# A causal penalty that waits in PSUM: ScalarE presets the diagonal blocks, and the scores come in three pieces

## The chip, the core and the metric

The kernel runs on one core of a Trainium2 chip. Its time is the device time of one execution in microseconds (us). The engines are named as in the profile: PE is TensorE (PEld its weight loads), DVE is VectorE, ACT is ScalarE, POOL is GpSimd, and SP issues most of the DMAs. A weight load and its product are two records each for a 32-bit product, because such a product runs in two passes; a 16-bit product and a transpose run in one.

## What is computed

The input x is 4 sequences of 512 tokens with 128 features. A first block adds ordinary causal attention to it, and six layers of local attention with feed-forward parts follow. The change touches only the first block:

```python
x = x + attn(layernorm(x), Wq, Wk, Wv, Wr)
# inside attn: 16 heads of 64
scores = SCALE * einsum('bqhd,bkhd->bhqk', q, k)
causal = triu(ones((s, s)), k=1)
scores = scores + MASK_PENALTY * causal        # -50 where key > query
attn = softmax(scores, axis=-1)
out = einsum('bhqk,bkhd->bqhd', attn, v)       # then @ Wr
```

The penalty is finite, so keys ahead of the query keep a small weight and all 512 keys are scored for each query.

## The kernel before

**Tiles and slots.** The first stage works on row blocks. A block (class `Rows`) is one sequence `b`, one pair of heads `c` (8 pairs) and one quarter `t` of the queries (4 quarters of 128): 128 blocks in all, each a PSUM tile `ps_sc` of 128 x 2 heads x 512 keys in 32 bit, which fills two banks. There are two such tiles (`bufs=2`), so block n writes the tile that block n-2 had. A loop over `m` handles two blocks in each of 64 slots: even slots have the quarters 0 and 1, odd slots the quarters 2 and 3. The order on every engine is the order of the calls in this loop (lines 422 to 493), written out by hand.

**A slot on PE.** (1) `times_v1` (L393): attention times v, half of it for an older pair of heads, from m = 4 on. (2) `scores` for both blocks (L308): for each block two halves of 256 keys by two heads, each head on its own 64 rows of the array; the two heads' products run beside each other. (3) `penalty` (L323): for each block and head one 16-bit product of an identity (`ident16`) with the mask `pen` adds the penalty to the block's own 128 x 128 square, the only one that the diagonal crosses. (4) In odd slots `make_v` (L287). (5) `transposes` (L373) of the first block of the slot before, 4 for each head. (6) `make_q` (L271, even) or `make_k` (L277, odd). (7) The transposes of the second block of the slot before. The q, k and v products and the layer norm share the one bank `ps_pj`.

**The other engines in a slot.** DVE takes the row maximum of a block over all 512 keys (L335, 128x1024), and a second bias for the squares behind the diagonal, whose penalty is constant (`bias`, L339; not for quarter 3). ACT takes the exponents (L348): for each head the keys up to the diagonal square, and the rest with the other bias; each is followed by a read of the accumulated sum. POOL normalises (L362). ACT copies the first head's transposes to SBUF and DVE the second's (L377, L381). ACT also copies v (L294) and q (L273), DVE copies k (L279) and, in odd slots, the finished head pair `aT` (L403).

ACT's order in a slot is: v (odd slots), first block's transposes of the slot before, exponents of the first block, exponents of the second, q (even slots), the second block's transposes of the slot before. DVE's is: `aT` (odd slots), first maximum, its bias, transposes, second maximum, its bias, k (odd slots), sums and reciprocals.

**Even slots with more work.** For the layer norm of the next sequence and of the residual, even slots hold a mean (L109, L111, L113), a variance (L118, L120) or a scaling (L126, L130): six slots of each kind. Thirteen even slots from m = 8 on hold none of these and are called plain here. Three odd slots also hold a projection of 16 products (L407).

**The start.** SP issues the loads of x's first half, `ident16`, `pen`, then x of the second sequence (L200), and further loads; wq, wk and wv are issued by ACT. PE transposes the second sequence (`load_x(1)`, L224) before 16 warming products (L239) and the first q.

Only these calls of the loop matter for what follows, in this order:

```python
times_v1(g // NC, g % NC, odd)           # m >= 4
for r in now: r.scores()
for r in now: r.penalty()
now[0].maximum()                         # then v, norm steps, bias
old[0].transposes()
now[0].exponents()                       # then now[1].maximum(), bias
now[1].exponents()                       # then the copies of q and of the transposes
```

Of the kernel before, what the change touches and what calls it, by code (L numbers as in the profile page):

```python
# [8 lines left out]
F32 = mybir.dt.float32  # L9
# [6 lines left out]
P = 128  # L16
# [4 lines left out]
NC = INNER // P  # L21
# [11 lines left out]
def body(ctx: ExitStack, tc: tile.TileContext, a, out: bass.AP):  # L33
# [5 lines left out]
    nc = tc.nc  # L39
    x = a["x"]  # L40
    B, S, _ = x.shape
# [18 lines left out]
    tabs = const.tile([P, NT, 4, HD], F32, tag="tabs", name="tabs")  # L60
    band = const.tile([P, 2, 2 * W], BF16, tag="band", name="band")
    ident16 = const.tile([P, P], BF16, tag="ident16", name="ident16")
# [99 lines left out]
    s1 = steps[0].enter_context(tc.tile_pool(name="s1", bufs=1))  # L162
    ps1t = steps[0].enter_context(tc.tile_pool(name="ps1t", bufs=1, space=PSUM, side="right"))
    ps1 = step0.enter_context(tc.tile_pool(name="ps1", bufs=1, space=PSUM))
# [25 lines left out]
    with tc.manual_schedule():  # L190
# [2 lines left out]
        wv = s1.tile([P, INNER], F32, tag="wv", name="wv")  # L193
        wr = s1c.tile([P, NC, EMB], F32, tag="wr", name="wr")
        pen = s1.tile([P, P], BF16, tag="pen", name="pen")
        xr = [s1.tile([P, NT, EMB], F32, tag="xr", name=f"xr{b}", bufs=2) for b in range(B)]
        for b in range(B):
            src = x[b].rearrange("(t p) e -> p t e", p=P)
            if b:
                nc.sync.dma_start(out=xr[b], in_=src)  # L200
            else:
                nc.sync.dma_start(out=xr[b][:, 0:2], in_=src[:, 0:2])
                nc.scalar.dma_start(out=xr[b][:, 2:NT], in_=src[:, 2:NT])
                nc.sync.dma_start(out=ident16, in_=a["ident16"])
                nc.sync.dma_start(out=pen, in_=a["pen"])
        for t_, n_ in ((wq, "wq"), (wk, "wk"), (wv, "wv")):
            nc.scalar.dma_start(out=t_, in_=a[n_])
        nc.sync.dma_start(out=wr, in_=a["wr"].rearrange("(c p) e -> p c e", p=P))
# [58 lines left out]
        qs, ks, vs, pTs, os_, aTs = {}, {}, {}, {}, {}, {}  # L267
# [28 lines left out]
        class Rows:  # L296


            def __init__(self, b, c, t):
                self.b, self.c, self.t = b, c, t  # L300

            def scores(self):
                b, c, t = self.b, self.c, self.t
                sc = self.sc = ps1.tile([P, 2, S], F32, tag="sc", name="ps_sc", bufs=2)
                for k0 in range(0, S, S // 2):
                    for h in range(2):
                        rows = slice(h * HD, (h + 1) * HD)
                        mm(  # L308
                            sc[:, h, k0 : k0 + S // 2],
                            lhsT=qs[b, c][rows, t * P : (t + 1) * P],  # L310
                            rhs=ks[b, c][rows, k0 : k0 + S // 2],
                            start=(k0 == 0),
                            stop=False,
                            skip_group_check=True,
                        )

# [67 lines left out]
        def times_v1(b, c, half):  # L384

            if half == 0:
                os_[b, c] = ps1b.tile([P, S], F32, tag="o1", name="ps_o1", bufs=1)
            o = os_[b, c]
            for k in (2 * half, 2 * half + 1):
                for h in range(2):  # L390
                    col = (2 * c + h) % HEADS * HD
                    j, col = col // 512, col % 512
                    mm(  # L393
                        o[h * HD : (h + 1) * HD, :],
                        lhsT=vs[b, j][:, k, col : col + HD],
                        rhs=pTs[b, c][:, h, k, :],
                        start=(k == 0),
                        stop=(k == NT - 1),
                        skip_group_check=True,
                    )  # L400
            if half == 1:
                at = aTs[b, c] = s1c.tile([P, S], F32, tag="aT1", name="aT1", bufs=NC + 2)
                nc.vector.tensor_copy(at, o)  # L403

        def project_out1(b, y):
            for c in range(NC):
# [5 lines left out]
        rows = [Rows(b, c, t) for b in range(B) for c in range(NC) for t in range(NT)]  # L412
# [8 lines left out]
        last = len(rows) // 2  # L421
        for m in range(last):
            b, c, odd = m // (2 * NC), m // 2 % NC, m % 2
            now = rows[2 * m : 2 * m + 2]
            old = rows[2 * m - 2 : 2 * m] if m else []
            if m >= 4:
                g = m // 2 - 2
                times_v1(g // NC, g % NC, odd)
            for r in now:
                r.scores()  # L430
            for r in now:
                r.penalty()
            if m in (2, 3):
                load_x(m)

            scale = None
            if not odd and c == 3 and b + 1 < B:
                scale = norms[b + 1][2]
            if b in range(1, B) and not odd and c == 6:
                scale = norms1[b - 1][2]  # L440
            if scale:
                scale()
            if now:
                now[0].maximum()
            if m < 2:
                make_v(0, 0, 2 * m)
                make_v(0, 0, 2 * m + 1)
            if odd and c < NT:
                make_v(b, 1, c)
            elif odd and b + 1 < B:  # L450
                make_v(b + 1, 0, c - NT)
            if not odd and 1 <= c <= 2 and b + 1 < B:
                if c == 1:
                    norms[b + 1] = norm_x(b + 1)
                norms[b + 1][c - 1]()
            if b in range(1, B) and not odd and 4 <= c <= 5:
                norms1[b - 1][c - 4]()
            if now:
                now[0].bias()
            if old:  # L460
                old[0].transposes()
            out_ = b > 0 and c == 1 and odd
            if now:
                now[0].exponents()
                if not out_:
                    now[1].maximum()
                    now[1].bias()

            bn, cn = (b, c + 1) if c + 1 < NC else (b + 1, 0)
            copies = []  # L470
            if bn < B:
                copies.append((make_k if odd else make_q)(bn, cn))
            if out_ and now:
                now[1].maximum()
                now[1].bias()
            if now:
                now[0].inverse()
                now[0].normalise()
            if old:
                copies.append(old[1].transposes(later=True))  # L480
            if now:
                now[1].exponents()
            for f in copies:
                f()
            if now:
                now[1].inverse()
                now[1].normalise()
            if out_:
                y = bank1()
                project_out1(b - 1, y)  # L490
                residual1(b - 1, y)
                norms1[b - 1] = norm_x1(bank1, b - 1)
            if b == B - 1 and c == 2 and not odd:
                start = shifted(0), layer_tables(0)
# [393 lines left out]
    def first_slot():  # L888


        new = units[0]
        part[0] = 2
        times_v1(B - 1, NC - 2, 0)
        do_project(new, 0)
        do_project(new, 1)
        rows[-2].transposes()
        rows[-1].transposes(later=True)()
        first_step()
        square(new, 0)
        times_v1(B - 1, NC - 2, 1)  # L900
        rotate(new, 0)
        sum_squares(new, 0)
        add_rotated(new, 0)
        times_v1(B - 1, NC - 1, 0)
        square(new, 1)
        rotate(new, 1)
        sum_squares(new, 1)
        add_rotated(new, 1)
        guard(new)
        nc.scalar.preload_act_table_set("natural_log_exp_and_others")  # L910
        inverse_norms(new)
        times_v1(B - 1, NC - 1, 1)
        second_step()
        over_norm(new, 0)
        over_norm(new, 1)
        do_project(new, 2)
        keep_v(new)
# [89 lines left out]
    with tc.manual_schedule():  # L1007
# [14 lines left out]
        for n in range(NT, end - NT, NT):  # L1022
            f = Ffn(units[n - 1], eng=nc.gpsimd, later=later)
# [26 lines left out]
        last = Ffn(units[end - 1], NT - 1, 1, big, sixths, nc.gpsimd)  # L1050
# [53 lines left out]
def _constants(n):  # L1104
# [4 lines left out]
    f = np.float32  # L1109
    half = np.arange(0, HD, 2, dtype=f)  # L1110
    inv_freq = (f(1.0) / np.power(f(10000.0), half / f(HD))).astype(f)
    t = np.arange(n, dtype=f)
# [8 lines left out]
    def by_token(lo, hi):  # L1121
# [3 lines left out]
    tabs = np.stack(  # L1125
        [
            by_token(cos * scale, cos * scale) * f(8.0),
            by_token(-sin * scale, sin * scale) * f(8.0),
            by_token(cos * inv, cos * inv),
            by_token(-sin * inv, sin * inv),  # L1130
        ],
        axis=2,
    )

    q = np.arange(W)[:, None]
    k = np.arange(2 * W)[None, :] - W
    seen = (q >= k) & (q <= k + W)
    band = np.zeros((P, 2, 2 * W), f)
# [3 lines left out]
    band = band.astype(ml_dtypes.bfloat16)  # L1142
# [1 line left out]
    pen = np.where(np.arange(P)[None, :] > np.arange(P)[:, None], PEN, 0.0).astype(ml_dtypes.bfloat16)  # L1144
    ident16 = np.eye(P).astype(ml_dtypes.bfloat16)
    zeros = np.zeros((W, 2, NC, HD + 1), f)
    return {"tabs": tabs, "band": band, "pen": pen, "ident16": ident16, "zeros": zeros}


# [49 lines left out]
```

## Time and profile before

| What | Value |
|---|---|
| Median of 3 runs | 2070.51 us (2067.06 to 2072.57) |
| The profiled execution: its own time | 2072.4 us |
| Its span, first to last instruction | 2070.6 us |
| Mean granted TensorE clock | 0.996 |
| PE busy in the span | 2028.4 us (98%) |
| ACT busy | 1368.2 us (66%) |
| DVE busy | 1640.8 us (79%) |
| POOL busy | 1316.5 us (64%) |
| First scores to last scores of the first stage | 23.5 us to 524.8 us |
| L323 (penalty) PE busy | 25.4 us, 256 records |
| L308 (scores) PE busy | 129.1 us, 1024 records |

PE's busy time counts a product's latency too, and products overlap, so a busy PE isn't at its peak. The profiled execution lies 1.8 us above its span and 1.9 us above the median of the runs.

### The profile page before, as it was taken

How to read it: one execution, taken by the hardware profiler on the slowest of the kernel's cores; microseconds unless marked ns; L12 is line 12 of the kernel's file. 1: busy time of each engine (PE TensorE's matmuls, PEld its weight loads, DVE VectorE, ACT ScalarE, POOL GpSimd, SP SyncE). 2: the span in 40 equal slices, each digit the busy share in tenths (PEclk: the TensorE clock that was granted, in tenths of full speed). 3: DMA queues.
4: the chain of work that ended last, by engine and by line, in shares of the span. 5: the costliest groups of instructions: out<-in, count | busy, mean ns of one | idle time of the engine just before them, and what ended most of it. 6: DMA issues, size and time to landing. Idle time of an engine off the chain costs nothing.

```text
span 2070.6 us, 77263 instructions
## 1 busy us (share of the span) xinstructions
PE 2028.4 (98%) x34382; PEld 1329.1 (64%) x34382; DVE 1640.8 (79%) x2240; ACT 1368.2 (66%) x2678; POOL 1316.5 (64%) x1432
## 2 busy tenths in 40 slices
PE   7999999999999999999999999999999999999998
PEld 5665555655466666666666666666666666666665
DVE  3766766767698888888888888888888888888885
ACT  3665665666455766676776676776667776677763
POOL 1554554555677677667767667667677767667762
PEclk8999999999999999999999999999999999999999
DMA  3000000000011121111211112111121111211110
GB/s 127 1 1 1 1 1 1 1 1 1 12 44 36 42 67 44 44 44 33 77 44 34 54 36 64 53 35 44 46 64 44 38 51 46 67 41 44 38 45 27
DMA packets 34968, 77.44 MB, mean 37 GB/s; under 512 B 4686, under 2 KB 18764, under 8 KB 34636
## 3 DMA queue, kind: packets, MB, share of 16 engines
q1 hardware_dynamic: 33932, 70.79, 11.8%
q8 instruction: 272, 4.46, 0.9%
q10 hardware_dynamic: 704, 1.70, 0.2%
q14 instruction: 60, 0.49, 0.1%
HBM read 23.50 MB, written 1.05 MB: 12 GB/s over the span
## 4 chain that ended last, share of the span: by engine, by line
PE 91%; DVE 5%; ACT 2%; POOL 1%; issue 1%; DMA 0%; SPq 0%; POOLq 0%; ACTq 0%
PE ps_proj L548 23%; PE ps_one L661 12%; PE ps_one L762 7%; PE ps_att L737 7%; PE ps_sc L308 6%; PE ps_o L393 6%; PE ps_att L700 5%; PE ps_pt L373 5%; PE ps_proj L812 3%; PE ps_proj L813 3%; PE ps_proj L832 3%; PE ps_pj L287 1%; PE ps_att L690 1%; PE ps_pj L277 1%; PE ps_pj L271 1%; PE ps_pj L407 1%
## 5 line engine op out<-in xcount | busy, mean ns | idle before, releaser
L587 POOL TENSOR_TENSOR rot<-rot,t 128x1024 f32<-128x1024 f32 x192 | 454.2, 2366 | 232.6 <-DVE t L576 220.1
L548 PE MATMUL ps_proj<-wqkv,xs 128*128 128x512 f32 x1152 | 569.0, 602 | 0.5 <-PE ps_one L661 0.2
L362 POOL TENSOR_TENSOR pr<-pr,den 128x1024 f32<-128x1024 f32 x128 | 241.0, 1893 | 248.3 <-DVE den L359 238.5
L606 POOL TENSOR_TENSOR rot<-rot,ss 128x1024 f32<-128x1024 f32 x192 | 361.3, 1903 | 7.4
L560 ACT ACTIVATE sq<-ps_proj 128x1024 f32<-128x1024 f32 x192 | 196.4, 1023 | 93.8 <-PE ps_proj L548 93.6
L548 PEld LDWEIGHTS ps_proj<-wqkv,xs 128*128 128x128 f32 x1152 | 188.2, 190 | 102.0 <-issue 92.1
L570 DVE TENSOR_TENSOR rot<-ps_proj,lt 128x1024 f32<-128x1024 f32 x192 | 233.3, 1215 | 10.2 <-ACT sq L560 10.0
L576 DVE TENSOR_TENSOR t<-ps_proj,lt 128x1024 f32<-128x1024 f32 x192 | 232.9, 1213 | 0.0
L348 ACT ACTIVATE pr<-ps_sc,nm 128x128 f32<-128x128 f32 (+3 forms) x448 | 220.3, 509 | 11.8 <-DVE nm L335 8.6
L565 DVE TENSOR_REDUCE ss<-sq 128x16 f32<-128x1024 f32 x192 | 221.1, 1190 | 0.0
L661 PEld LDWEIGHTS ps_one<-ident,rot 128*128 128x128 f32 x1536 | 172.7, 141 | 61.2 <-issue 51.2
L661 PE MATMUL ps_one<-ident,rot 128*128 128x128 f32 x1536 | 205.1, 276 | 1.1 <-POOL xs L170 0.6
L335 DVE TENSOR_REDUCE nm<-ps_sc 128x2 f32<-128x1024 f32 x128 | 155.9, 1218 | 62.9 <-PE ps_sc L323 62.8
L664 ACT COPY pT<-ps_one 128x512 f32<-128x512 f32 x192 | 110.0, 587 | 136.6 <-PE ps_one L661 136.6
L762 PEld LDWEIGHTS ps_one<-aT,wo 128*128 128x128 f32 x1536 | 182.9, 192 | 23.6 <-issue 17.7
L762 PE MATMUL ps_one<-aT,wo 128*128 128x128 f32 x1536 | 189.1, 276 | 0.3 <-ACT tmp_t L852 0.2
L746 DVE RECIPROCAL rden<-ps_att 128x8 f32<-128x8 f32 x192 | 38.8, 202 | 176.8 <-PE ps_att L737 176.7
L648 ACT COPY vt<-ps_proj 128x512 f32<-128x512 f32 x192 | 103.1, 590 | 96.4 <-PE ps_proj L548 96.4
L373 PEld LDWEIGHTS ps_pt<-ident,pr 128*128 128x128 f32 x1024 | 117.4, 142 | 58.5 <-issue 47.4
L664 ACT COPY qT<-ps_one 128x512 f32<-128x512 f32 x192 | 103.1, 589 | 66.1 <-PE ps_one L661 66.1
L377 ACT COPY pT<-ps_pt 128x512 f32<-128x512 f32 x128 | 75.6, 591 | 98.0 <-PE ps_pt L373 98.0
L373 PE MATMUL ps_pt<-ident,pr 128*128 128x128 f32 x1024 | 135.9, 274 | 3.0 <-DVE pT L381 2.4
(178 smaller groups left out, 3763.2 us busy)
## 6 DMA issues: line engine op xcount, KB each, us to landing
vs<-vt SPq DMA_DIRECT2D x96, 390.0 KB, 3.7
vs<-vt SPq DMA_DIRECT2D x72, 130.0 KB, 3.6
wqkv<-in_wqkv_dram SPq DMA_DIRECT2D x18, 512.0 KB, 4.0
vs<-in_zeros_dram SPq DMA_DIRECT2D x24, 130.0 KB, 3.7
wo<-in_wo_dram SPq DMA_DIRECT2D x6, 512.0 KB, 4.2
w<-in_w_dram SPq DMA_DIRECT2D x6, 341.0 KB, 5.9
xr<-in_x_dram SPq DMA_DIRECT2D x3, 256.0 KB, 7.6
scales<-in_scales_dram SPq DMA_DIRECT2D x6, 128.0 KB, 3.1
```

Source lines behind the costliest of these rows:

```text
L348: nc.scalar.activation(self.pr[:, h, cols], self.sc[:, h, cols], AF.Exp, bias=self.nm[:, part_, h : h + 1], accum_out=self.den[:, part_, h ...
L362: nc.gpsimd.tensor_tensor(self.pr, self.pr, self.den[:, 0].unsqueeze(2).to_broadcast([P, 2, S]), ALU.mult)
L373: nc.tensor.transpose(pt[:, k * P : (k + 1) * P], self.pr[:, h, k * P : (k + 1) * P], ident)
L548: mm(p[:, c, :], lhsT=u.xs[:, u.T * P : (u.T + 1) * P], rhs=wpart[j][:, c * 512 : (c + 1) * 512], start=True, stop=True,)
L565: nc.vector.tensor_reduce(u.ss[:, j * HEADS : (j + 1) * HEADS], heads(u.sq[j]), AX.X, ALU.add)
L570: nc.vector.tensor_tensor(heads(t0), heads(pf), lt[:, u.T, 2 * j].unsqueeze(1).to_broadcast([P, HEADS, HD]), ALU.mult)
L576: nc.vector.tensor_tensor(t1.rearrange("p (h t d) -> p h t d", t=2, d=half), pf.rearrange("p (h t d) -> p h t d", t=2, d=half)[:, :, ::-1, :],
L587: nc.gpsimd.tensor_tensor(u.r[j], u.r[j], u.t1, ALU.add)
L606: nc.gpsimd.tensor_tensor(heads(u.r[j]), heads(u.r[j]), u.ss[:, j * HEADS : (j + 1) * HEADS].unsqueeze(2).to_broadcast([P, HEADS, HD]), AL ...
L661: nc.tensor.transpose(tp[:, c * P : (c + 1) * P], src[:, (4 * g + c) * P : (4 * g + c + 1) * P], ident)
L664: nc.scalar.copy(dst[:, 4 * g : 4 * g + 4, col0 : col0 + P], tp.rearrange("p (c t) -> p c t", c=4))
L762: mm(y[:, 0:P], lhsT=wo_w[0][:, k, :], rhs=u.aT[:, g].rearrange("p (j f) -> p j f", f=P)[:, :, f0 : f0 + W], start=(k == 0), stop=(k == NC ...
```

## The change

A 32-bit copy of the mask, `pen32`, is loaded by SP right after `pen`, ahead of x of the second sequence. From the second slot on, ACT copies it into the own square of both heads of a block's PSUM tile (`preset`, one instruction of 128x256 for each block) one slot ahead: for the first block of the next slot right after the exponents of the first block of this slot, and the same for the second. Both take the tile whose exponents ACT has just read. The scores then start with the own square, adding to what lies there, and go on with the two squares of the other half of the keys and the square beside the own one: pieces of 128, 256 and 128 keys, instead of 256 and 256. The 16-bit products stay in the first slot (m = 0) only, whose scores are also in three pieces. In odd slots the copy of `aT` moves behind the first maximum on DVE. The file's second half is unchanged but for a call of the function that `times_v1` now returns.

```diff
+        pen32 = s1.tile([P, P], F32, tag="pen32", name="pen32")
...
                 nc.sync.dma_start(out=pen, in_=a["pen"])
+                nc.sync.dma_start(out=pen32, in_=a["pen32"])
...
-                self.b, self.c, self.t = b, c, t
+                self.b, self.c, self.t, self.sc = b, c, t, None
+
+            def preset(self):
+                sc = self.sc = ps1.tile([P, 2, S], F32, tag="sc", name="ps_sc", bufs=2)
+                nc.scalar.copy(
+                    sc[:, :, self.t * P : (self.t + 1) * P], pen32.unsqueeze(1).to_broadcast([P, 2, P])
+                )
 
             def scores(self):
                 b, c, t = self.b, self.c, self.t
-                sc = self.sc = ps1.tile([P, 2, S], F32, tag="sc", name="ps_sc", bufs=2)
-                for k0 in range(0, S, S // 2):
+                own = self.sc is not None
+                if not own:
+                    self.sc = ps1.tile([P, 2, S], F32, tag="sc", name="ps_sc", bufs=2)
+                sc, far = self.sc, (1 - t // 2) * 2
+                for k, (k0, n) in enumerate(((t, 1), (far, 2), (t ^ 1, 1))):
+                    cols = slice(k0 * P, (k0 + n) * P)
                     for h in range(2):
                         rows = slice(h * HD, (h + 1) * HD)
                         mm(
-                            sc[:, h, k0 : k0 + S // 2],
+                            sc[:, h, cols],
                             lhsT=qs[b, c][rows, t * P : (t + 1) * P],
-                            rhs=ks[b, c][rows, k0 : k0 + S // 2],
-                            start=(k0 == 0),
-                            stop=False,
+                            rhs=ks[b, c][rows, cols],
+                            start=(k == own),
+                            stop=own or k == 2,
                             skip_group_check=True,
                         )
...
             if half == 1:
                 at = aTs[b, c] = s1c.tile([P, S], F32, tag="aT1", name="aT1", bufs=NC + 2)
-                nc.vector.tensor_copy(at, o)
+                return lambda: nc.vector.tensor_copy(at, o)
+            return lambda: None
...
-                times_v1(g // NC, g % NC, odd)
+                keep = times_v1(g // NC, g % NC, odd)
             for r in now:
                 r.scores()
-            for r in now:
+            for r in now if m == 0 else ():
                 r.penalty()
...
             if now:
                 now[0].maximum()
+            if m >= 4:
+                keep()
...
                 now[0].exponents()
+                if m + 1 < last:
+                    rows[2 * m + 2].preset()
...
                 now[1].exponents()
+                if m + 1 < last:
+                    rows[2 * m + 3].preset()
```

## The prediction

> **What bounds the kernel now.** The page first: one engine is nearly full.
>
> ```profile
> PE 2028.4 (98%) x34382; PEld 1329.1 (64%) x34382; DVE 1640.8 (79%) x2240; ACT 1368.2 (66%) x2678; POOL 1316.5 (64%) x1432
> ```
>
> Busy is not bound, so the second view is the busy time by stretches of 14.50 us, one even and one odd plain slot.
>
> ```profile
> 99.21:113.71 14.50, 14.50 (x96) 8.79 (x95) 10.46 (x21) 10.14 (x34) 7.88 (x5) 1.00 0.01 2
> ```
>
> PE has no gap, at full clock; ACT (fifth figure) has 4.4 us to spare. The timeline of PE shows the steps: scores, penalty and transposes start when the step before lets them.
>
> ```profile
> 104.25 2.00 PE L308 MATMUL ps_sc<-k,q 64*128 64x256 f32 x16
> 106.19 0.40 PE L323 MATMUL ps_sc<-pen,ident 128*128 128x128 bf16 x4
> 106.42 1.04 PE L373 MATMUL ps_pt<-ident,pr 128*128 128x128 f32 x8
> ...
> 111.04 2.00 PE L308 MATMUL ps_sc<-k,q 64*128 64x256 f32 x16
> 112.97 0.40 PE L323 MATMUL ps_sc<-pen,ident 128*128 128x128 bf16 x4
> 113.20 0.65 PE L287 MATMUL ps_pj<-wv,xnT 128*128 128x512 f32 x1
> ```
>
> ACT's timeline of the same even slot runs late: the exponents end at 111.70, after the next scores have begun at 111.04.
>
> ```profile
> 107.06 0.58 ACT L377 COPY pT<-ps_pt 128x512 f32<-128x512 f32 x1 [2.52 <-PE ps_pt L373]
> 107.83 0.37 ACT L348 ACTIVATE pr<-ps_sc,nm 128x128 f32<-128x128 f32 x1 [0.18 <-DVE nm L335]
> ...
> 109.55 0.21 ACT L348 ACTIVATION_READ_ACCUMULATOR pr<-ps_sc,nm 128x1 f32 x1
> 109.77 0.47 ACT L348 ACTIVATE pr<-ps_sc,nm 128x256 f32<-128x256 f32 x1
> ...
> 111.49 0.21 ACT L348 ACTIVATION_READ_ACCUMULATOR pr<-ps_sc,nm 128x1 f32 x1
> ```
>
> Those scores' second block needs the tile that these exponents read. After an even slot with a mean the timeline shows the wait:
>
> ```profile
> 170.18 2.13 PE L308 MATMUL ps_sc<-k,q 64*128 64x256 f32 x16
> 170.87 0.24 ACT L348 ACTIVATION_READ_ACCUMULATOR pr<-ps_sc,nm 128x1 f32 x1
> 171.17 0.73 PEld L308 LDWEIGHTS ps_sc<-k,q 64*128 64x128 f32 x8 [0.26 <-ACT pr L348]
> ```
>
> The load starts 0.05 after the read's end, 0.99 after the first score, and the scores take 2.13, not 2.00. So a load up to 0.86 after the first score costs nothing. The plain slot is ready at 111.70 + 0.05 = 111.75 against 111.04 + 0.86 = 111.90: a slack of 0.15, which is what the change spends.
>
> **PE: the penalty goes.** In even slots the penalty's first load starts at 106.18 and the transposes at 106.42: 0.24. Without it their own load, hidden now behind the penalty, lies open: 0.05, by L393, whose loads are as long (136 ns against 142) and whose first product of a group takes 645 ns, not 592. Saved: 0.19. In odd slots v follows 0.23 after the penalty's load, its second record comes 0.06 later than spacing asks, and an open load of 128 32-bit columns costs 0.11 (first score 481 ns, others 376): 0.18. At 0.19, over 63 slots, **-12.0 us**.
>
> **PE: three pieces.** The columns stay the same, but four record steps of a block are 128 wide. Their price is that of a step whose weights change each time:
>
> ```profile
> 1009.51 1.95 PE L762 MATMUL ps_one<-aT,wo 128*128 128x128 f32 x16
> ```
>
> The steps there are 0.11 apart, the load hidden, against 0.215 for 256 columns: 0 to 0.02 us more for a block; I take 0.01, 128 times: **+1.3**. The Trainium skill, "TensorE: Matmul & The Clock Gate", section "The mechanism", speaks against the pieces: a weight load overlaps running products only in another row group. By it a narrow step would be load plus stream, 0.21, and the sum 55 us worse; the row above shows the overlap within one row group.
>
> **ACT: the preset's price.** No row has ACT writing PSUM. The nearest are copies from SBUF:
>
> ```profile
> L804 ACT COPY rot<-xT x1: 298/298/298, 2048.6 to 2048.6; 64x128 f32<-64x128 f32 x1
> ```
>
> With 107 ns for 128 more columns (L113 takes 310 ns at 128 and 524 at 384) that is 0.40; it holds ACT for 0.31, as instructions overlap by 0.09. The farthest rows are 0.23 (128x32) and 0.68 (512-wide exponents). The Trainium skill, "ScalarE: Activation LUTs", section "Step-by-step: what each stage is for", says that ACT reaches PSUM faster than SBUF, without a figure; every 0.1 us saved would take 6.6 us off the sum below.
>
> The preset also waits for ACT's own last read: in the changed kernel's instruction list it carries a wait on ACT. Such a wait costs 0.03:
>
> ```profile
> 607.63 0.23 ACT L598 ACTIVATE y<-ss 128x32 f32<-128x32 f32 x1 [2.47 <-POOL ss L590]
> 607.89 0.23 ACT L599 ACTIVATE y<-y 128x32 f32<-128x32 f32 x1
> ```
>
> So a preset delays what is queued behind it: after a read's start ACT goes on at 0.21 + 0.03 + 0.31 = 0.55 instead of 0.09: +0.46. And PE is released by the second preset's end, 0.03 + 0.40 = 0.43 later than by the read.
>
> **The plain even slot.** The first maximum no longer waits for both blocks and the penalty: it starts about 1.2 after the first score, not 2.25. The first exponents then wait only for the copy of the transposes (107.06, 0.19 earlier) and its 0.48: 107.35, so 0.48 earlier. The second exponents gain 0.48, lose 0.46, and lose a wait of 0.14 for their bias (109.64 to 109.77), whose maximum comes earlier too: 0.16 earlier. Ready: 111.75 - 0.16 + 0.43 = 112.02. Needed: 111.90 - 0.19 = 111.71. **PE stalls 0.31**, in the odd slot that follows.
>
> The same sum for the others, each from its own slack:
> - Variance (6): slack 0.44, exponents only 0.19 earlier, bias wait 0.09: 0.19 - 0.46 + 0.09 makes them 0.18 later; stall 0.18 + 0.43 + 0.19 - 0.44 = 0.36.
> - Scaling (6): L130 still precedes the maximum, so 0.19 earlier; bias wait 0.14, 0.13 later, slack 0.15: stall 0.60.
> - Mean (5): the exponents come 0.30 earlier, as L111 no longer follows a late maximum; 0.16 later, no slack, 0.13 lost already: 0.78 added.
> - The first three slots wait for ACT already: 0.87 added each.
>
> Sum: 13 x 0.31 + 6 x 0.36 + 6 x 0.60 + 5 x 0.78 + 2.6 = **+16.3**.
>
> Odd slots: their exponents end at 118.57 and the next slot's scores start at 118.76, so the second block's load has a slack of 118.76 + 0.86 - 118.62 = 1.00. The 0.19 and the stall move both sides, since the first exponents there follow v and the transposes; 0.46 + 0.43 leave 0.11, no stall. If that cover is gone, each 0.1 costs 3 us.
>
> **Edits at nothing.** Behind the second preset lie the copies of q and of transposes; q is copied about 0.5 us before v needs its bank. The `aT` copy moves ahead of the first bias in odd slots: 0.67, but that bias is ready 0.8 before ACT asks (ACT waits for v there); its bank is next written after the following slot has begun. POOL starts an even slot's second block at 112.67 for 1.89, 1.4 before its transposes at 115.92, and moves by under 0.5; an odd slot's second waits for its first on POOL anyway (118.05 to 121.79, transposes at 122.7).
>
> **The start.** `pen32` goes ahead of the second sequence on SP. PE waits 3.96 us for that load now, and it stays ahead of warming and q. One issue costs 0.45, its 64 KB 0.2 of the DMA flow: 0.2 to 0.7, I take **+0.5**.
>
> **Sum:** -12.0 + 1.3 + 16.3 + 0.5 = +6.1 on the profiled execution's 2072.4 (span 2070.6): 2078.5. That execution lies 1.9 above the median, so 2076.6.
>
> **Rivals.**
> - *The preset is covered* (faster): ACT has 4.4 us free in 14.5 and four presets ask 1.8; if release came 0.31 earlier, PE would stay the bound: -12.0 + 1.3 + 0.5 = -10.2, 2060.3. Against it: the free time lies after the exponents, the slack was 0.15, and 2.13 at 170.18 shows the wait. It needs a release within 0.1 us of the read.
> - *The preset is dear* (slower): a PSUM write as slow as the 512-wide exponents, 0.68, adds 0.28 twice in 33 slots: +18.5, 2095. It decides from 0.41 on. Against it: copies are cheaper than exponents.
> - *Narrow loads lie open* (slower): 4 x 128 steps at 0.107 are +55, while a slower PE takes 12 to 16 us of stalls away: about 2117. Against it: the 0.11 steps.
> - Whether PE adds to the preset or overwrites it changes no time.
>
> **The numbers.** A measurement of this kernel tells 0.3%, or 6.2 us, from no change. The forecast has 0.74; presets of 0.34 to 0.45, steps and start at their ends put it at 2070 to 2084, half beyond 6.2: slower 0.37, same 0.37. Covered: 0.13, faster. Dear: 0.08; open loads: 0.05, both slower. Faster 0.13, same 0.37, slower 0.50. The range takes in the covered case and ends at 2085.
>
> **What would show it.** Right: 126 presets of 0.40; the penalty left in the first slot alone; score steps of 0.11; the first maximum 1.2 after the first score; odd slots whose second block waits for the preset, 0.3 after plain slots, 0.6 after scalings and 0.9 after means; even slots without a wait. Wrong: two plain slots in 14.12 (covered), scores over 2.3 without a wait (open loads), waits in even slots.

## The result, and the profile after

The changed kernel takes 2080.07 us (median of 8 runs, 2076.15 to 2083.36) against 2070.41 for the kernel before beside it (8 runs, 2067.06 to 2075.39): a ratio of 1.0042, 95% interval 1.0027 to 1.0056. It is slower, by 5.6 to 11.6 us (the interval times 2070.41). The prediction had 2076.6 in a range of 2059 to 2085, with "slower" as the likeliest of the three outcomes. The profiled execution took 2081.23 us, its span is 2079.4, and its mean granted clock 0.993 (before: 0.996).

The page after shows what became of the chain that ended last. Before, PE had 91% of it and ACT 2%:

```profile
PE 2029.2 (98%) x34642; PEld 1343.3 (65%) x34642; DVE 1640.6 (79%) x2240; ACT 1415.8 (68%) x2804; POOL 1316.5 (63%) x1432
...
PE 83%; ACT 8%; DVE 5%; issue 1%; POOL 1%; DMA 0%; SPq 0%; POOLq 0%; ACTq 0%
```

PE's busy time did not fall, although 252 products left it, for rows like the 2.36 and the half clock below count as busy. ACT's share of the chain is the new thing. The windows of the same kind of two plain slots as before (one even, one odd) give 14.47 us, where before had 14.50:

```profile
111.84:126.31 14.47, 14.40 (x104) 9.06 (x102) 10.57 (x20) 11.57 (x39) 7.53 (x5) 1.00 0.01 1
```

The timeline of PE in those slots answers to the rows of L308, L323 and L373 before. The penalty is gone and the transposes start 1.96 behind the first score; the odd slot's scores take 2.36 (second fence), not the 2.02 of the even slot:

```profile
111.84 2.02 PE L322 MATMUL ps_sc<-k,q 64*128 64x128 f32 x24
113.80 1.09 PE L387 MATMUL ps_pt<-ident,pr 128*128 128x128 f32 x8
114.72 1.02 PE L273 MATMUL ps_pj<-xnT,wq 128*128 128x512 f32 x2
115.58 1.04 PE L387 MATMUL ps_pt<-ident,pr 128*128 128x128 f32 x8
```

```profile
118.42 2.36 PE L322 MATMUL ps_sc<-k,q 64*128 64x128 f32 x24
```

ACT's timeline and PE's weight loads there show why. The last read ends at 118.97 + 0.21 = 119.18, the preset starts 0.03 later and ends at 119.21 + 0.38 = 119.59, and the second block's first load follows at 119.63:

```profile
116.69 0.22 ACT L362 ACTIVATION_READ_ACCUMULATOR pr<-ps_sc,nm 128x1 f32 x1
116.94 0.38 ACT L308 COPY ps_sc<-pen 128x256 f32<-128x256 f32 x1
117.25 0.47 ACT L362 ACTIVATE pr<-ps_sc,nm 128x256 f32<-128x256 f32 x1
...
118.97 0.21 ACT L362 ACTIVATION_READ_ACCUMULATOR pr<-ps_sc,nm 128x1 f32 x1
119.21 0.38 ACT L308 COPY ps_sc<-pen 128x256 f32<-128x256 f32 x1
```

```profile
118.42 0.96 PEld L322 LDWEIGHTS ps_sc<-k,q 64*128 64x128 f32 x12 [0.81 <-issue]
119.63 0.96 PEld L322 LDWEIGHTS ps_sc<-k,q 64*128 64x128 f32 x12 [0.26 <-ACT ps_sc L308]
```

The rows at 116.94 and 117.25 show the first half of the mechanism as well: the first preset stands in ACT's queue ahead of the second block's exponents. After an even slot with a mean, where the row before read 2.13, PE's timeline has a break of 0.67:

```profile
177.49 1.15 PE L322 MATMUL ps_sc<-k,q 64*128 64x128 f32 x12
179.30 1.15 PE L322 MATMUL ps_sc<-k,q 64*128 64x128 f32 x12 [0.67 <-ACT ps_sc L308]
```

So the predicted mechanism is there. A second thing is there that the prediction did not have. The windows of the first slots, before and then after (the figure behind the five engines' busy times is the granted clock):

```profile
20.00:25.00 5.00, 4.12 (x18) 2.22 (x18) 0.69 (x1) 0.60 (x1) 0.00 (x0) 0.79 0.33 117
25.00:30.00 5.00, 3.65 (x16) 1.15 (x12) 2.69 (x4) 2.03 (x7) 0.00 (x0) 1.00 0.00 0
...
55.00:60.00 5.00, 5.00 (x32) 2.81 (x32) 3.41 (x7) 4.05 (x14) 1.95 (x2) 1.00 0.00 0
```

```profile
20.00:25.00 5.00, 4.12 (x13) 1.96 (x13) 0.69 (x1) 0.60 (x1) 0.00 (x0) 0.50 0.34 110
25.00:30.00 5.00, 4.33 (x25) 3.06 (x22) 2.25 (x3) 0.59 (x1) 0.00 (x0) 0.67 0.00 0
...
55.00:60.00 5.00, 3.95 (x18) 3.04 (x19) 2.40 (x4) 2.56 (x8) 2.75 (x2) 0.56 0.02 5
60.00:65.00 5.00, 5.00 (x24) 3.26 (x24) 2.39 (x4) 3.77 (x12) 0.00 (x0) 0.76 0.00 0
```

Before, the clock rises to full at 22.1 us and stays there through the stage; after, it rises at 28.3 and falls to half once more from 55.6 to 62.4. Taken by the starts of the scores, the two profiled executions differ like this:

| Part of the span | Before | After | Difference | The prediction's sum for it |
|---|---|---|---|---|
| up to the first score | 23.47 | 23.56 | +0.09 | +0.5 |
| slot 0 | 7.55 | 10.22 | +2.67 | 0 |
| slots 1 to 3 | 27.73 | 32.32 | +4.59 | +2.1 |
| slots 4 to 62 | 464.43 | 466.71 | +2.28 | +3.4 |
| slot 63 to the end | 1547.40 | 1546.60 | -0.80 | +0.1 |
| span | 2070.58 | 2079.41 | +8.83 | +6.1 |

### The profile page after: what moved, and what is told of

The parts are those of the page before. It is cut to its first block, busy times and chain, and to the rows that moved or that the text cites. A ratio compares the mean times of both kernels' runs of the same rounds, so it can differ in the third digit from the quotient of the medians.

```text
span 2079.4 us, 77913 instructions
## 1 busy us (share of the span) xinstructions
PE 2029.2 (98%) x34642; PEld 1343.3 (65%) x34642; DVE 1640.6 (79%) x2240; ACT 1415.8 (68%) x2804; POOL 1316.5 (63%) x1432
## 4 chain that ended last, share of the span: by engine, by line
PE 83%; ACT 8%; DVE 5%; issue 1%; POOL 1%; DMA 0%; SPq 0%; POOLq 0%; ACTq 0%
PE ps_proj L569 23%; PE ps_one L682 12%; PE ps_one L783 7%; PE ps_att L758 7%; ACT pr L362 6%; PE ps_att L721 5%; PE ps_sc L322 5%; PE ps_o L407 3%; PE ps_pt L387 3%; PE ps_proj L833 3%; PE ps_proj L834 3%; PE ps_proj L853 3%; PE ps_pj L289 2%; PE ps_att L711 1%; PE ps_pj L279 1%
## 5 line engine op out<-in xcount | busy, mean ns | idle before, releaser
L322 PEld LDWEIGHTS ps_sc<-k,q 64*128 64x128 f32 x1536 | 116.7, 190 | 77.3 <-issue 40.6
L322 PE MATMUL ps_sc<-k,q 64*128 64x128 f32 (+1 forms) x1536 | 141.2, 324 | 13.7 <-ACT ps_sc L308 10.7
```

The costliest lines, as they stand in the source:

```text
L322: mm(sc[:, h, cols], lhsT=qs[b, c][rows, t * P : (t + 1) * P], rhs=ks[b, c][rows, cols], start=(k == own), stop=own or k == 2, skip_group_ ...
```

## The experiments

**1. The narrow steps alone (e_pieces).** The kernel before, its scores in three pieces, the penalty products kept:

```diff
-                for k0 in range(0, S, S // 2):
+                for k, (k0, n) in enumerate(((t, 1), (far, 2), (t ^ 1, 1))):
+                    cols = slice(k0 * P, (k0 + n) * P)
```

> The kernel before with its scores in three pieces and the penalty products kept: the narrow steps alone. My theory: the 128-wide steps are about 0.11 us apart with the load hidden, so 0 to +2.5 us against before, and the same waits as before. Rival (narrow loads lie open): each of the 4 narrow steps of a block costs about 0.1 us more, scores of 2.4 us a slot, and +40 to +55 us.

2072.03 us against 2071.43 (ratio 1.0004, 0.9995 to 1.0012): +0.6, -1.0 to +2.5. Two plain slots take 14.56 instead of 14.50, which is 0.028 for a slot and, over slots 4 to 62, +1.49 (464.43 to 465.92). The narrow loads are not open. The rival would have made +40 to +55. The sentence of the Trainium skill that the prediction weighed ("TensorE: Matmul & The Clock Gate", section "The mechanism": a weight load overlaps running products only in another row group) gave +55 by the prediction's estimate; the measurement decides against that for this form of product.

**2. The products' worth (e_nopen).** The kernel before without `penalty`; it leaves the causal penalty out.

```diff
-            for r in now:
-                r.penalty()
```

> The kernel before without its penalty products (it leaves the causal penalty out): what the removed products were worth. My theory: 0.19 us a slot over 64 slots, -12 us against before, two plain slots in 14.12 us instead of 14.50, no new waits of PE. Rival (their time was hidden, or another engine becomes the bound at once): 0 to -4 us.

2059.24 us against 2071.43 (0.9942, 0.9930 to 0.9955): -12.2, -14.5 to -9.3. Two plain slots take 14.08:

```profile
101.76:115.84 14.08, 14.08 (x89) 8.42 (x87) 10.92 (x21) 10.00 (x35) 7.53 (x5) 1.00 0.00 0
```

That is 0.42 for two slots; slots 4 to 62 shrink by 11.75. PE does get this time when nothing takes it back, so the first term of the sum was right, and the gain was lost elsewhere.

**3. The suspected cost doubled (e_double).** Each preset is issued twice:

```diff
-                nc.scalar.copy(
+                for _ in range(2):
+                    nc.scalar.copy(
...
```

> The changed kernel with every preset issued twice: the suspected cost doubled. My theory (the preset delays the release of the next even slot's and odd slot's second block through ACT's queue): each preset holds ACT 0.3 to 0.4 us more, two of them ahead of a second block, so 0.6 to 0.8 us more in each of about 31 odd slots, and the even slots, with 0.11 us of slack left, begin to wait too: +20 to +40 us against the changed kernel. Rival (ACT has time to spare and the preset is not on the path): within 2 us of the changed kernel.

2125.47 us, ratio 1.0265 (1.0250 to 1.0279) to the kernel before, some 45 above the changed kernel. That is more than expected, and the timelines say why. A second copy holds ACT for 0.40 (two take 0.78, one 0.38), and in a plain odd slot the second block's scores now start 0.82 later than after one preset (the wait grows from 0.337 to 1.154): both doubled presets pass to PE in full. Of the 30 even slots, which did not wait, 27 now wait some 0.65. Over slots 4 to 62 that makes 0.82 x 29 + 0.65 x 27 = 41, and they grew by 41.1 (466.7 to 507.8). The error of the expectation was to count the even slots at almost nothing.

```profile
109.22 0.21 ACT L363 ACTIVATION_READ_ACCUMULATOR pr<-ps_sc,nm 128x1 f32 x1
109.46 0.78 ACT L309 COPY ps_sc<-pen 128x256 f32<-128x256 f32 x2
```

```profile
108.27 1.15 PE L323 MATMUL ps_sc<-k,q 64*128 64x128 f32 x12
110.30 1.15 PE L323 MATMUL ps_sc<-k,q 64*128 64x128 f32 x12 [0.88 <-ACT ps_sc L309]
```

That ACT has free time in a slot does not help: it has it at another place in the slot. The rival "preset covered" falls here.

**4. The presets without the start (e_late).** Penalty products in the first four slots, presets from the fifth on:

```diff
-            for r in now if m == 0 else ():
+            for r in now if m < 4 else ():
                 r.penalty()
...
-                if m + 1 < last:
+                if 3 <= m < last - 1:
                     rows[2 * m + 2].preset()
```

> The changed kernel with penalty products in the first four slots and presets from the fifth slot on: the start as before, the rest as changed. Theory A (the presets' waits in the first slots cost the start 7 us, 2.6 of them as stalls and the rest as a low granted clock that PE's idle gaps bring): slot 4 begins as in the kernel before, the clock does not go back to half after 25 us, and the time is 4 to 7 us less than the changed kernel's. Theory B (the low clock of that trace is chance of the execution and has nothing to do with the presets): only the stalls go, 1 to 3 us less. Theory C (the cost is in the later slots): within 1 us of the changed kernel.

2074.12 us against 2071.43 (1.0013, 1.0004 to 1.0022): +2.7, about 6 less than the changed kernel. Slots 4 to 62 take 466.84, as in the changed kernel (466.71), so the later slots are worth +2.4 and the start the rest. Theory C falls. The windows show what of the clock goes and what stays:

```profile
20.00:25.00 5.00, 4.12 (x12) 1.78 (x12) 0.69 (x1) 0.60 (x1) 0.00 (x0) 0.50 0.32 113
25.00:30.00 5.00, 4.33 (x27) 3.11 (x24) 1.94 (x3) 0.59 (x1) 0.00 (x0) 0.67 0.02 3
...
55.00:60.00 5.00, 5.00 (x36) 3.33 (x36) 3.77 (x5) 3.68 (x12) 1.90 (x1) 1.00 0.00 2
```

The second fall is gone, the late first rise is not. So theory A fits the one and not the other.

**5. The start alone (e_early).** The opposite half: presets for slots 1 to 3, products from the fourth slot on.

```diff
-            for r in now if m == 0 else ():
+            for r in now if m == 0 or m >= 4 else ():
                 r.penalty()
...
-                if m + 1 < last:
+                if m < 3:
                     rows[2 * m + 2].preset()
```

> The opposite half: the changed kernel with presets for slots 1, 2 and 3 alone and penalty products from the fourth slot on, so the start as changed and the rest as before. Theory A (the start costs what the sum lacked): the profile shows a stretch of half clock of 3.4 or 6.8 us between 30 and 63 us, as the four kernels with presets from slot 1 on do and the five with products in the first slots and the kernel before do not; 4 to 7 us more than the kernel before (the early load 0.8, the pieces 0.6, stalls about 1.5, clock 1.7 to 3.4), later slots without waits for a preset. Theory C (the start is as cheap as in the sum, 2 to 3 us, and that clock was chance): no such stretch, 2 to 3 us more.

2080.67 us against 2071.50 (1.0046, 1.0033 to 1.0060): +9.2, 6.8 to 12.4. The expectation missed twice: the time is more, and the profile shows no second fall. What its profile has is +4.2 up to slot 4 (the first rise late, at 27.7 us; slots 1 to 3 take 29.34, which is 1.55 over the 27.79 of e_late: what the waits cost there, less what the absent products save, without a fall of the clock), +2.6 in slots 4 to 62 and +1.8 behind them. Of the 2.6, the pieces are 1.5, and 1.1 is in slots 57, 59 and 61, where e_pieces has 7.05, 6.95 and 6.81 and this kernel 7.39, 7.28 and 7.28. There the moved copy `aT` (L417) shows a price: with the products kept, the maximum waits for the penalty and the copy stands behind it, so DVE reaches the copy of the transposes late and PE waits. DVE's and PE's timelines of slot 59:

```profile
503.00 1.23 DVE L349 TENSOR_REDUCE nm<-ps_sc 128x2 f32<-128x1024 f32 x1 [0.52 <-PE ps_sc L337]
504.14 0.68 DVE L417 COPY aT<-ps_o 128x512 f32<-128x512 f32 x1
```

```profile
505.55 0.66 PE L387 MATMUL ps_pt<-ident,pr 128*128 128x128 f32 x4 [0.28 <-DVE pT L395]
```

In the changed kernel the maximum is early: from 480 to 540 us PE's weight loads wait once for DVE's copy of the transposes (0.6 us in all), in e_early six times (3.4 us). The 1.8 behind the stage (half clock for 6.8 us at 2035 where most profiles have 3.4) was not followed further.

**6. The first preset on another engine (e_dve0).** The first block's preset goes to VectorE behind `inverse`, the second's stays on ScalarE:

```diff
                 now[0].exponents()
-                if m + 1 < last:
-                    rows[2 * m + 2].preset()
...
                 now[0].inverse()
+                if m + 1 < last:
+                    rows[2 * m + 2].preset(nc.vector.tensor_copy)
```

> The changed kernel with the first block's preset on VectorE, the second's left on ScalarE. My theory (the first preset delays the second exponents by 0.46 in ACT's queue, and that delay passes to PE): PE's waits for the second preset fall by 0.46, so none after plain and variance slots, about 0.1 after scalings and 0.45 after means; the time is 9 to 13 us less than the changed kernel's, so 0 to 4 below the kernel before. Rival (the second preset's own 0.38 before PE's release is what counts, not its place in the queue): the waits stay as they are, within 2 us of the changed kernel.

2068.43 us against 2071.87 (0.9986, 0.9977 to 0.9995): -3.4, and 11.6 below the changed kernel. Two plain slots take 14.14. The second exponents follow the first without the gap of a preset, and the odd slot's scores are back at 2.02 (ACT's and then PE's timeline):

```profile
110.94 0.22 ACT L362 ACTIVATION_READ_ACCUMULATOR pr<-ps_sc,nm 128x1 f32 x1
111.11 0.47 ACT L362 ACTIVATE pr<-ps_sc,nm 128x256 f32<-128x256 f32 x1
```

```profile
112.67 2.02 PE L322 MATMUL ps_sc<-k,q 64*128 64x128 f32 x24
```

The waits that are left: none after variance slots and plain slots (but 0.25 after two late plain ones), 0.25 after scalings (expected 0.1), 0.47 after means (expected 0.45). The waits in slots 4 to 63 sum to 4.6 here against 14.9 in the changed kernel; slots 4 to 62 take 457.42, which is 9.3 less than in the changed kernel and 7.0 less than before. So the place of the first preset in ACT's queue, not the second preset's own length, is what turned the gain of these slots into a loss.

**7. Both presets on VectorE (e_dve01).** As e_dve0, and the second block's preset on VectorE as well, behind the second exponents:

```diff
                 now[1].exponents()
                 if m + 1 < last:
-                    rows[2 * m + 3].preset()
+                    rows[2 * m + 3].preset(nc.vector.tensor_copy)
```

> The changed kernel with both presets on VectorE, the second right behind the second exponents. My theory: the first as before 0.46 earlier; the second waits for another engine's release (0.05 in place of 0.03) and costs about 0.35 to 0.45 there, so PE's waits are those of the kernel with one preset on VectorE, within 0.1 us a slot; the time within 3 us of it. Rival (VectorE, 79% busy, reaches the second preset late): waits of 0.5 us or more come back in the odd slots, +15 us or more.

2069.46 us (0.9989, 0.9980 to 0.9998), slots 4 to 62 in 458.12: the waits are longer than in e_dve0 by 0.02 after plain slots and 0.06 after means. Which engine writes the second preset matters little.

**8. The place of the load (e_late_dma).** As e_late, with the load of `pen32` behind that of `wr`, not ahead of the second sequence:

```diff
-                nc.sync.dma_start(out=pen32, in_=a["pen32"])
...
         nc.sync.dma_start(out=wr, in_=a["wr"].rearrange("(c p) e -> p c e", p=P))
+        nc.sync.dma_start(out=pen32, in_=a["pen32"])
```

> The changed kernel with penalty products in the first four slots, and the load of the 32-bit penalty at the end of SP's first loads instead of ahead of the second sequence: the DMA's place alone, against the same kernel with the early load. My sum's step: 0.2 to 0.7 us less, by an earlier load of the second sequence. Theory B for the start (the first rise of the granted clock, at 22 us in the kernel before and at 28 in the changed one, is where a window happens to fall and does not hang on that load): the rise can be at either place. Theory A (the load's delay moves the rise by a whole window): the rise is at 22 us again and the time 2.5 to 3 us less.

2072.33 us against 2071.87 (1.0004, 0.9995 to 1.0013), where e_late had 1.0013: the two intervals overlap, so its time does not settle the step. The profiles say more together. PE's first transposes of the second sequence start at 9.54 to 10.23 us, 9.85 on average, in the six profiles with the early load, and at 8.15 to 9.83, 8.95 on average, in the five without it (the kernel before is the 9.83). By these averages the load costs about 0.9, where the prediction took 0.5; the figure is rough, as the two groups overlap. The pair of before and after, +0.09 at the first score, hid it by chance. The clock rose at 20.5 us in this run, but at 27.2 in e_best, whose load is as late: the rise does not hang on the load alone. Four of the six profiles with the early load rise late and one of the five without it; whether the load shifts the odds, so few do not tell.

**9. All of it together (e_best).** e_dve0 with the first four slots of e_late and the load of e_late_dma.

> The kernel with one preset on VectorE, with the start put right as well: penalty products in the first four slots, presets from the fifth on, and the load of the 32-bit penalty at the end of SP's first loads. Sum by my theory: -12.2 x 60/63 for the products, +0.6 for the pieces, about +3 for the waits left after scalings and means: 8 us less than the kernel before, 2063. Rival (each gain is lost to another wait, on VectorE or on PE's other inputs): within 3 us of the kernel before.

2061.58 us against 2071.87 (0.9953, 0.9940 to 0.9965): -10.3, -12.4 to -7.3. It beats both kernels. The expectation was -8, and its parts are there: slots 4 to 62 in 457.27 (-7.2), waits of 4.4 in the stage, and no fall of the clock in slots 1 to 3.

## Why the prediction was right, and where its sum was off

**The penalty's 0.19** held: 0.42 for two plain slots in e_nopen, -11.75 in slots 4 to 62 against a predicted -11.2.

**The pieces' 0.01** for a block measured 0.014, +1.5 in the stage against +1.2.

**The preset** was taken as 0.40 and takes 0.376 (all 126 within 2 ns), and the wait on ACT's own read is 0.03, as taken. The first maximum starts 1.20 behind the first score, as said.

**The waits** of the second block held term by term. Predicted and measured, in the slot behind: plain 0.31 and 0.34; variance 0.36 and 0.34; scaling 0.60 and 0.57; mean 0.91 (with the 0.13 of before) and 0.93. Even slots have none. The slots pair by pair follow: a plain pair -0.03 (predicted -0.38 + 0.04 + 0.31 = -0.03), a pair with a variance +0.02 (+0.02), with a scaling +0.25 (+0.26), with a mean +0.41 (+0.44). The last slots (54 to 62) are shorter by some 0.9 in all than these terms make them; why was not followed.

The waits of the changed kernel from 60 to 540 us carry the reading. Columns: who waited for whom, total us, times, longest. Before, its two rows were the release by the exponents (24.0 us) and the maximum's wait for the penalty (58.0 us):

```profile
PEld ps_sc L322 <- ACT ps_sc L308: 22.2, 42, 0.9
...
DVE nm L349 <- PE ps_sc L322: 21.3, 24, 2.3
...
PE ps_sc L322 <- ACT ps_sc L308: 5.5, 12, 0.7
```

**The start is the step that was mis-sized.** The sum gave it 0.5 for the load and 0.87 for each of three slots, which is 2.6 in all once the products that go are taken off, at a full clock. Measured in the same way, the waits of slots 1 to 3 cost 1.55 at full clock (e_early over e_late), slot 1's first block waits 0.4 longer before that (1.11 against 0.71 in e_late's timeline), and the load costs about 0.9: 2.9, near the 2.6 of the sum. What was missing is the clock, a term that the sum had at nothing. In the changed kernel's profile half a clock for 6.8 us inside slot 3 makes slots 1 to 3 take 32.32 against 29.34 in e_early, which has the same instructions there: +3.0. The late first rise makes slot 0 longer by about 2.1 (9.65 in e_late against 7.58 in e_late_dma, which have the same instructions there), in this profile and in those of e_late, e_early, e_double and e_best, whose first score comes at half clock. Those two are 5.1 of the 8.8 us. Without them the pair differs by 3.7, less than the 6.1 of the sum, as slots 4 to 62 and what follows came out 2.0 cheaper together than the sum had them. So that the median lies only 3.5 us above the forecast is in part luck: the two errors have opposite signs.

How often this comes is only partly settled. Five kernels preset slots 1 to 3, and four of their five profiles (the changed kernel, e_double, e_dve0, e_dve01) show a further fall between 32 and 63 us; none of the six without presets there does. In them PE waits more than 1 us before a block, again and again, as in the changed kernel's timeline:

```profile
53.78 1.15 PE L322 MATMUL ps_sc<-k,q 64*128 64x128 f32 x12 [1.34 <-ACT ps_sc L308]
56.05 1.23 PE L322 MATMUL ps_sc<-k,q 64*128 64x128 f32 x6 [1.12 <-ACT ps_sc L308]
```

Within a profile the changes of the clock lie whole multiples of 3.41 us apart, which gives a grid of windows, and the busy time of PE in each window says more (the first figure behind the length). First the window ahead of the fall in the changed kernel, then the emptiest one of e_early between the first rise and 65 us; e_early has the same waits, but they lie otherwise on its grid and no fall follows:

```profile
52.18:55.59 3.41, 1.41 (x15) 0.94 (x13) 1.27 (x5) 3.38 (x14) 1.62 (x1) 1.00 0.02 5
```

```profile
51.59:55.00 3.41, 1.87 (x19) 1.39 (x17) 1.72 (x5) 3.38 (x16) 1.17 (x1) 1.00 0.00 0
```

PE is busy for 0.41 of the first and 0.55 of the second. Ahead of the five falls of those four profiles the share is 0.41 to 0.49; the six kernels without presets there have no window under 0.59 between the first rise and 65 us. A window under a half is not always followed by a fall (e_double has one of 0.49 that is not), and no run sets this share by itself: that the waits bring the fall by emptying a window is argued from these profiles, not shown by an experiment. No run shows the late first rise to be an effect of the presets: six profiles rise at 20.5 to 22.7 us, five at 27.1 to 28.3, and both groups hold kernels with the early and the late load. The eight runs of the changed kernel agree with a clock that differs from one to the next: spans of 2074.3 and 2074.6 at a mean clock of 0.996, of 2080.8 and 2081.6 at 0.991 and 0.992. Against the 2070.6 of the kernel before, whose clock was 0.996, the first two are 4 us more, and the last two 10 to 11.

**The rivals.** *Covered* failed for the reason given against it: PE takes the tile within 0.05 of the release. e_dve0 shows what its condition is worth, a plain pair of 14.14. *Dear* and *open loads* failed by their own rows, 0.376 and 0.11.

## What to carry to other kernels

Work that is taken from a full engine and given to a half-idle one is paid where it lands in that engine's queue: ahead of the instruction that releases a buffer it costs its whole length, once the slack is spent (0.82 us for two more copies of 0.40 in e_double); on a third engine it cost far less (4.6 us of waits in e_dve0 against 14.9). Look for the slack of the release, not for the share of busy time, and subtract it slot by slot, for each kind of slot. And count the first iterations, where nothing covers a wait, separately: waits of over 1 us on TensorE there went with a fall of its clock in four profiles of five.

## What the runs showed of the hardware

- ScalarE's copy of 128 x 256 32-bit values from SBUF into PSUM takes 376 ns, VectorE's 407 (e_dve0, 63 of each). ACT starts its next instruction 0.31 behind the preset's start, and a second copy into the same place 0.40 behind.
- The granted clock moved between 1.0 and 0.5 alone, and its low stretches that end inside the span last, in the eleven profiles, 3.41, 6.83, 10.24, 13.65, 17.07 or 20.48 us: multiples of 3.41. Each of the five falls between the first rise and 65 us follows a stretch of 3.41 us in which PE is busy for 0.41 to 0.49 of the time.
- Scores of a block in three pieces, with twelve weight loads and products in place of eight, take 0.014 us longer (e_pieces); a narrow step hides its load as a wide one does: steps of 128 columns are 0.11 apart there, with loads of 0.19.
